# Attending in one accumulation bank, a longer rest in the gating, and key features made in blocks of 432 keys

## The chip, the core and the metric

The kernel runs on one core of a Trainium2 chip. The metric is the device time of one execution in microseconds (us). A core has five engines that run their own instruction streams: TensorE (PE, with its weight loads shown apart as PEld), VectorE (DVE), ScalarE (ACT), GpSimd (POOL) and SyncE (SP, which issues the transfers here). Matmuls write into PSUM, eight banks of 512 fp32 columns by 128 partitions; everything is fp32.

## What is computed

Eight images of 128 channels and 36 x 36 = 1296 positions go through two layers. The first is a convolutional attention with residual. The second is an additive attention over the 1296 tokens, followed by a layer of 64 experts which each take the 8 tokens they rate highest.

```python
def _L1_attn_ref(x, mask, Wq, bq, Wk, bk, w, bw):
    q = jnp.einsum('bld,ed->ble', x, Wq) + bq
    k = jnp.einsum('bld,ed->ble', x, Wk) + bk
    t = jnp.tanh(q[:, :, None, :] + k[:, None, :, :])
    scores = jnp.einsum('bijd,d->bij', t, w) + bw[0]
    attn = jax.nn.softmax(scores, axis=-1)
    return jnp.einsum('bij,bjd->bid', attn, x)
...
x = x + _L0_conv_ref(_gn(x), ...)
t = _to_tokens(x)
t = t + _L1_attn_ref(_ln_t(t), ...)
t = t + _L1_ffn_ref(_ln_t(t), ...)
```

The score of a query i and a key j is a sum over 128 channels of w times tanh(q + k). It isn't computed channel by channel. The kernel writes tanh through products of exponentials: over small groups of channels, a query and a key each get features exp(...), and the sum over a group is a quotient of two matrix products of these features.

## The kernel before

**The loop.** A *unit* is one key tile of 128 keys (11 tiles, the last of 16 keys) against one chunk of 432 queries (three chunks), for one image (called a batch here). A full unit has 12 *slots*, the unit of the 16-key tile has two; in all there are 2928 slots. A slot p does, in this order:

- `numerators(p)`: two products `n` into two banks of the PSUM pool `ps_n` (four banks);
- `denominators(p + 3)`: two products `d` into one of two pairs of banks of `ps_d`, then a Ln on ACT, and in every second slot an Exp over two slots' logarithms `lq` (the reciprocals);
- `terms(p)`: DVE multiplies `n` by `lq`. In slots 2, 5, 8 and 11 (`DVE_PAIRS`) DVE also adds the products up, in PSUM; in the other slots they go to SBUF as `rp`, and POOL adds them up.

Of three slots, two have products of 32 rows and the third (k = 2, 5, 8, 11) of 64 rows. The two halves of `n`, or of `d`, lie on different rows of the array.

**The work beside it.** Everything else is written as generators that stand in four lanes: `first_of_all` (features of queries, the scores of the 16-key tile), `urgent` (attending), `gates` (the expert gating of the batch before) and `background` (the next batch's first layer, its tokens and its key features). Each generator yields at the points where it may be interrupted: `matmuls(rest)` means that its next piece issues matmuls, and that it isn't taken up before `rest` slots have passed; `TAKE` means that its next piece takes a result out of PSUM, from the next slot on. `take_turns` runs pieces without matmuls at the start of a slot, except in `DVE_PAIRS` slots. `matmul_turn` runs at most one piece with matmuls at the end of a slot, and for the lanes other than `first_of_all` none in a slot just before a `DVE_PAIRS` slot, nor while the columns issued so far are ahead of 400 per slot (`PACE`). So the lanes get at most two turns in three slots. All of these take their PSUM banks from `ps_n` too, through `aux`. A bank is given out again in the program's order, and who gets it waits for its last reader. `exps` runs the `urgent` lane until it is empty when a chunk has its first exponentials and is about to get its second.

**Key features.** `keys` (L667) makes, for each key tile, eight matmuls of 128 columns (`NF` = 8), four to a bank, so two turns a tile; each bank gets one Exp of 512 columns on ACT (L687) into a tile `ks` (three buffers) and one write to the DRAM tensor `kd`, which holds a tile's features contiguously. For the 16-key tile POOL makes two masked copies (L692). `prefetch` (L932) loads a key tile's features as 4096 contiguous bytes per partition, two units ahead. In batch 0 the first tile is made before the loop straight into SBUF, two more tiles follow, and the others stand in the `urgent` lane.

**Attending.** When a chunk has all its exponentials `e`, `attend` forms the weighted sum over the 1296 keys for its four blocks of 108 queries: 11 matmuls a block. They are split into six and five. The first six go into a bank that DVE copies into SBUF (`sums`, L770), the other five into another bank, and DVE adds the two (L772). Then come a reciprocal, a scaling with addition (L775), and the statistics for the next normalization. For the very last chunk `attend_early` does nine of the eleven in the same way ahead of time.

**Gating.** `gate_logits` normalizes the tokens: DVE adds the epsilon (`ve`), two slots later POOL computes the inverse root `t_rs` (L265). Then come four transposes, a copy (L820), a rest of one slot, and two pairs of transposes back, which DVE scales with `t_rs` (L830).

Of the kernel before, what the change touches and what calls it, by code (L numbers as in the profile page):

```python
# [10 lines left out]
F32 = mybir.dt.float32  # L11
AF = mybir.ActivationFunctionType
ALU = mybir.AluOpType
# [3 lines left out]
N = H * W  # L17
# [53 lines left out]
def kernel(  # L71
# [41 lines left out]
        return t  # L113


    kd = [dram.tile([NKT, 128, NF * 128], F32, tag=f"kd{b % 2}", name=f"kd{b}") for b in range(NB)]
    tokd = [dram.tile([N, C], F32, tag=f"tokd{b % 2}", name=f"tokd{b}") for b in range(NB)]
    t2d = [dram.tile([C, N], F32, tag=f"t2d{b}", name=f"t2d{b}") for b in range(NB)]
    gd = [dram.tile([E, N], F32, tag=f"gd{b}", name=f"gd{b}") for b in range(NB)]
# [10 lines left out]
    with ExitStack() as loop, ExitStack() as score:  # L130
# [146 lines left out]
        def matmuls(rest=0):  # L277
            return (True, rest)
# [308 lines left out]
        prepared, made = {}, set()  # L587

        def tokens(b):

# [73 lines left out]
                nc.sync.dma_start(xr[32 * i : 32 * i + REM], xh[:REM, NKT - 1, :])  # L664
            prepared[b] = (xh, xT, xr)

        def keys(b, tiles):  # L667

            xT = prepared[b][1]
            yield matmuls(1)  # L670
            for t in tiles:
                o, n = KT[t]
                first = (b, t) == (0, order[0])
                if first:
                    kf_of[0] = kfp.tile([128, NF, 128], F32, tag="kf", name="kf")
                for q0 in (0, NF // 2):
                    some = slice(q0, q0 + NF // 2)
                    pk = aux("pk1").rearrange("p (q t) -> p q t", t=128)
                    for q in range(NF // 2):
                        bmm(pk[:, q, :n], a_k[:, (q0 + q) * 128 : (q0 + q + 1) * 128],  # L680
                           xT[:, o : o + n], start=True, stop=True)
                    yield TAKE
                    if first:
                        ks = kf_of[0][:, some, :]
                    else:
                        ks = kstp.tile([128, NF // 2, 128], F32, tag="ks", name="ks")
                    nc.scalar.activation(ks[:, :, :n], pk[:, :, :n], AF.Exp)  # L687
                    kd3 = kd[b][t].rearrange("p (q t) -> p q t", t=128)[:, some, :]
                    if n == REM:

                        for x in range(2):
                            nc.gpsimd.tensor_scalar(  # L692
                                ks[:, :, (x + 1) * n : (x + 2) * n], ks[:, :, :n],
                                pairs[:, min(q0, 1), x : x + 1], None, ALU.mult,
                            )
                        nc.sync.dma_start(kd3[:, :, : 2 * n], ks[:, :, n : 3 * n])
                    else:
                        nc.sync.dma_start(kd3, ks)
                    if q0 > 0:
                        made.add((b, t))  # L700
                    yield matmuls()

        def query_block(b, c, q, qf):

# [15 lines left out]
        def attend_early(b, c, es):  # L720

            xh, _, xr = prepared[b]
            held = [chunk_tile("sums") for _ in range(TPC // 2)]
            for i in range(TPC):
                at = (i % 2) * (C + 1)
                sums = early[i] = held[i // 2][:T, at : at + C + 1]
                for some in (order[:5], order[6 : NKT - 2] + order[5:6]):
                    pa = aux("pa1")[:T, : C + 1]
                    weigh(pa, i, some, es, xh, xr)
                    yield TAKE  # L730
                    if some[0] == order[0]:
                        nc.vector.tensor_copy(sums, pa)
                    else:
                        nc.vector.tensor_add(sums, pa, sums)
                    yield matmuls()

        def weigh(pa, i, some, es, xh, xr):

            for j in some:
                if j < NKT - 1:  # L740
                    e, v = es[j][:, i * T : (i + 1) * T], xh[:, j, :]
                else:
                    rows = slice(32 * i, 32 * i + REM)
                    e, v = es[j][rows, :T], xr[rows]
                bmm(pa, e, v, start=(j == some[0]), stop=(j == some[-1]))

        def attend(b, c, es):
# [11 lines left out]
            for i, at in enumerate(own):  # L759
                if i in early:  # L760
                    parts, sums = (order[NKT - 2 :],), early[i]
                else:
                    parts = (range(6), range(6, NKT))
                    sums = two.tile([T, C + 1], F32, tag="sums", name="sums")
                for some in parts:
                    pa = aux("pa1")[:T, : C + 1]
                    weigh(pa, i, some, es, xh, xr)
                    yield TAKE
                    if some[0] == 0:
                        nc.vector.tensor_copy(sums, pa)  # L770
                        yield matmuls()
                nc.vector.tensor_add(pa, pa, sums)  # L772
                inv = small.tile([T, 1], F32, tag="inv", name="inv")
                nc.vector.reciprocal(inv, pa[:, C : C + 1])
                nc.vector.scalar_tensor_tensor(  # L775
                    t2[:T, at, :], pa[:, :C], inv, t2[:T, at, :], ALU.mult, ALU.add
                )
                st = small.tile([T, 6], F32, tag="t2_st", name="t2_st")
                nc.vector.bn_stats(st, t2[:T, at, :])
                nc.vector.bn_aggr(mv[:, at, :], st)  # L780
                yield matmuls()
            if c == NCH - 1:
                prepared.pop(b)
            if b == NB - 1:
                yield from gate_logits(b, [c])
# [7 lines left out]
        def gate_logits(b, chunks):  # L793
# [23 lines left out]
            for c in chunks:  # L817
                tp, tt = turned(c, "t2T")
                yield TAKE
                nc.vector.tensor_copy(tt, tp[:, :CH])  # L820
                nc.sync.dma_start(t2d[b][:, c * CH : (c + 1) * CH], tt)
                yield matmuls(1)
                for j0 in range(0, TPC, 2):
                    tp = aux("tp3")
                    for j in (j0, j0 + 1):
                        turned_to(tp[:T, j * C : (j + 1) * C], tt[:, j * T : (j + 1) * T], ident)
                    yield TAKE
                    for j in (j0, j0 + 1):
                        t = c * TPC + j
                        nc.vector.tensor_scalar(  # L830
                            t2[:T, t, :], tp[:T, j * C : (j + 1) * C],
                            mv[:, t, 0:1], rs[:, t - tiles[0] : t - tiles[0] + 1],
                            ALU.subtract, ALU.mult,
                        )
                    yield matmuls()
# [90 lines left out]
        def prefetch(u):  # L926
            if u < len(units) and u not in kf_of:
                b, c, j = units[u]
                assert (b, j) in made
                n = 128 if j < NKT - 1 else 32  # L930
                kf = kfp.tile([128, NF, 128], F32, tag="kf", name="kf")
                nc.sync.dma_start(  # L932
                    kf[:, :, :n], kd[b][j].rearrange("p (q t) -> p q t", t=128)[:, :, :n]
                )
                kf_of[u] = kf

# [161 lines left out]
                next(aside, None)  # L1098
        drain(aside)
        a_q, a_k, cs_s, fb_s, eb_s = (feat[n] for n in ("a_q", "a_k", "cs_s", "fb_s", "eb_s"))  # L1100
        drain(tokens(0), keys(0, order[:1]))
        for i, q in enumerate(IN_TURN):
            if i < 3:
                drain(new_block(0, 0, q))
# [253 lines left out]
```

The softmax here doesn't subtract the row's maximum and nothing guards it: scores larger than these inputs give would overflow.

## Time and profile before

| | us |
|---|---|
| median of 3 runs (6137.38 to 6148.23) | 6137.45 |
| the profiled execution | 6140.74 |
| its span, first to last instruction | 6139.0 |
| POOL's additions `accp` of a slot (L1012), mean of one | 2.025 |
| DVE's products `rp` (L1003), mean of one | 0.600 |
| Exp of key features, 512 columns (L687), mean of one | 0.586 |
| Exp of key features, 64 columns (L687) | 0.205 |
| Exp of query features with bias, 432 columns (L710) | 0.608 |
| copy `sums` (L770), 92 of them | 0.289 |
| addition of `sums` (L772), 96 of them | 0.292 |

The loop's first slot starts about 162 us into the span and its last about 5985 us; the first layer of batch 0 lies ahead of it, and the experts' layer behind it. The mean granted clock of TensorE is 0.985 of full speed. The DMA engines are busy 13% of the time. A busy share is an average over the whole span; a line's last part names what ended the idle time ahead of its instructions.

### The profile page before, as it was taken

To read this page: it belongs to the slowest core of one execution; us is meant where nothing else is said; L and a number is where in the kernel's file an instruction comes from. 1 tells how busy PE (TensorE), PEld (TensorE's weight loads), DVE (VectorE), ACT (ScalarE), POOL (GpSimd) and SP (SyncE) were. 2 spreads that over 40 slices of the span, in tenths; PEclk is the share of its full clock that TensorE was granted. 3 is DMA by queue.
4 is the path that set the end of the run, shared out by engine and by line. 5 is a ranking of instruction groups with operands and counts; after the bars stand their busy time and mean duration, and the time that the engine had idled before them with its cause. 6 is when DMAs were issued, how large, how long until landed. Compare 5 with 4: busy or idle time off the path is not lost.

```text
span 6139.0 us, 93072 instructions
## 1 busy us (share of the span) xinstructions
PE 5957.9 (97%) x33480; PEld 2862.1 (47%) x33480; DVE 4796.4 (78%) x9521; ACT 5279.9 (86%) x5371; POOL 4597.7 (75%) x2819
## 2 busy tenths in 40 slices
PE   7999999999999999999999999999999999999996
PEld 5454444544544445444455444454444544544443
DVE  4787878877788787877888777887778877788882
ACT  1888898888988888889998889888898888999990
POOL 4777777777787777778778786877777777787870
PEclk9999999999999999999999999999999999999997
DMA  1210011100110002100111001110011100110008
GB/s 44 70 37 22 25 62 38 34 25 28 68 43 20 26 27 71 39 24 23 44 55 39 22 24 59 44 39 22 20 65 40 34 25 28 58 50 29 28 20 297
DMA packets 151519, 270.87 MB, mean 44 GB/s; under 512 B 45648, under 2 KB 76752, under 8 KB 151056
## 3 DMA queue, kind: packets, MB, share of 16 engines
q1 hardware_dynamic: 151056, 264.92, 13.0%
q8 instruction: 264, 4.33, 0.3%
q14 instruction: 199, 1.63, 0.1%
HBM read 200.41 MB, written 64.19 MB: 43 GB/s over the span
## 4 chain that ended last, share of the span: by engine, by line
PE 77%; ACT 7%; DVE 6%; issue 6%; POOL 2%; DMA 1%; SPq 0%; DVEq 0%; POOLq 0%; ACTq 0%
PE n L949 37%; PE d L949 12%; PE pa L284 7%; PE pc L284 5%; ACT lq L972 5%; PE s L284 3%; PE pk L284 3%; PE pq L284 3%; DVE rp L1003 2%; DVE n L997 1%; DVE accd L999 1%; PE d L954 1%; ACT lq L975 1%; DMA w<-in_weight_dram 1%; PE n L954 1%
## 5 line engine op out<-in xcount | busy, mean ns | idle before, releaser
L1012 POOL TENSOR_TENSOR accp<-accp,rp 128x864 f32<-128x864 f32 x1440 | 2915.8, 2025 | 1041.0 <-DVE rp L1003 948.8
L949 PE MATMUL n<-qf,kf 32*128 32x432 f32 (+1 forms) x11520 | 3325.3, 574 | 46.5 <-ACT e L1032 13.3
L949 PE MATMUL d<-qf,kf 32*128 32x432 f32 (+1 forms) x11520 | 2991.6, 561 | 38.7 <-ACT lq L972 38.2
L972 ACT ACTIVATE lq<-d 128x864 f32<-128x864 f32 x2928 | 2524.2, 878 | 542.6 <-PE d L949 512.1
L1003 DVE TENSOR_TENSOR rp<-n,lq 128x432 f32<-128x432 f32 x3912 | 2173.3, 600 | 743.5 <-PE d L949 542.8
L975 ACT ACTIVATE lq<-lq 128x1728 f32<-128x1728 f32 (+1 forms) x1464 | 2398.2, 1638 | 46.3
L949 PEld LDWEIGHTS n<-qf,kf 32*128 32x128 f32 (+1 forms) x11520 | 1206.4, 184 | 1600.3 <-DVE rp L1003 581.5
L949 PEld LDWEIGHTS d<-qf,kf 32*128 32x128 f32 (+1 forms) x11520 | 1090.0, 185 | 422.1 <-issue 224.7
L997 DVE TENSOR_TENSOR n<-n,lq 128x432 f32<-128x432 f32 x1440 | 814.9, 608 | 142.1 <-PE n L949 88.5
L999 DVE TENSOR_TENSOR accd<-n,accd 128x432 f32<-128x432 f32 x1440 | 866.3, 602 | 24.6
L1010 POOL TENSOR_TENSOR accp<-rp 128x864 f32<-128x864 f32 x240 | 485.2, 2022 | 197.7 <-DVE rp L1003 195.6
L711 POOL TENSOR_SCALAR qf<-qf,cs_s 128x432 f32<-128x432 f32 x192 | 260.9, 1365 | 45.0 <-ACT qf L710 44.4
L284 PEld LDWEIGHTS pa<-xh,e 128*108 128x108 f32 x1920 | 222.5, 174 | 131.1 <-DVE rp L1003 56.0
L1021 POOL TENSOR_TENSOR accd<-accp,accd 128x432 f32<-128x432 f32 x240 | 265.2, 1105 | 18.8
L1019 POOL TENSOR_TENSOR accp<-accp 128x432 f32<-128x432 f32 x240 | 264.4, 1102 | 16.7
L284 PE MATMUL pa<-xh,e 128*108 128x129 f32 x1920 | 262.9, 283 | 8.7 <-ACT e L1032 5.2
L284 PE MATMUL s<-q,k 128*116 128x432 f32 x480 | 230.3, 568 | 1.7 <-DVE q L316 1.4
L284 PEld LDWEIGHTS pk<-xT,a_k 128*128 128x128 f32 x1408 | 171.2, 192 | 107.0 <-DVE n L997 33.7
L462 POOL TENSOR_TENSOR tot<-tot,e 116x432 f32<-116x432 f32 x192 | 212.0, 1104 | 6.0 <-ACT e L471 4.6
L471 ACT ACTIVATE e<-s 116x432 f32<-116x432 f32 x240 | 124.9, 520 | 98.3 <-PE s L284 97.9
L284 PE MATMUL pa<-e,vw 116*128 116x432 f32 x480 | 204.6, 549 | 0.0
L284 PE MATMUL pk<-xT,a_k 128*128 128x128 f32 (+1 forms) x1408 | 202.5, 287 | 0.1
(213 smaller groups left out, 3788.4 us busy)
## 6 DMA issues: line engine op xcount, KB each, us to landing
kf<-kd SPq DMA_DIRECT2D x239, 512.0 KB
kd<-ks SPq DMA_DIRECT2D x158, 256.0 KB
w<-in_weight_dram SPq DMA_DIRECT2D x32, 1024.0 KB
wk_t<-wk_t_d SPq DMA_DIRECT2D x7, 768.0 KB
wv_t<-wv_t_d SPq DMA_DIRECT2D x7, 768.0 KB
wq_t<-wq_t_d SPq DMA_DIRECT2D x7, 768.0 KB
x<-in_x_dram SPq DMA_DIRECT2D x8, 648.0 KB
t<-tokd SPq DMA_DIRECT2D x96, 54.0 KB
```

What stands on the lines that cost most here:

```text
L284: mm(out, lhsT, rhs, **kw)
L711: nc.gpsimd.tensor_scalar(qf[:, 1, :], qf[:, 0, :], cs_s[:, q : q + 1], None, ALU.mult)
L949: mm(outs[h][:, :CH], kf[rows[h], q, :], qf_of[b, c, q][rows[h], part, :], start=True, stop=True)
L972: nc.scalar.activation(lq[:, o : o + n, :], d[:, :n, :CH], AF.Ln)
L975: nc.scalar.activation(some, some, AF.Exp, scale=-1.0)
L997: mult(ns[h], ns[h], lq[:, o + h, :])
L999: nc.vector.tensor_add(live["d"], ns[h], live["d"])
L1003: mult(rp[:, h, :], n, lq[:, o + h, :])
L1010: nc.gpsimd.tensor_add(live["p"], live["r"], rp)
L1012: nc.gpsimd.tensor_add(live["p"], live["p"], rp)
L1019: nc.gpsimd.tensor_add(s[:, 0, :], s[:, 0, :], s[:, 1, :])
L1021: nc.gpsimd.tensor_add(d, s[:, 0, :], d)
```

## The change

There are three edits.

1. Key features are made by `keys(b, lo, hi)` for a block of up to 432 keys: eight matmuls of the block's width, one to a bank, each a turn of its own with its own Exp and its own write. `kd` becomes `[128, NF, N]`, with the keys along the row, so that a tile's load has pieces of 512 bytes. The two masked copies of the last 16 keys are made per feature group into a tile `kr`, and go to a DRAM tensor of their own, `krd`. In batch 0 the blocks are 128, 384, 384, 16 and 384 keys.
2. Attending's 11 matmuls of a block accumulate in one bank, in turns of four, four and three; the bank is held from the first turn to the scaling. The copy and the addition of `sums` are gone (for the last chunk, early sums are copied once, and added once).
3. In the gating, the rest between the first chunk's copy and its transposes back is four slots instead of one (batch 7 excepted).

```diff
-    kd = [dram.tile([NKT, 128, NF * 128], F32, tag=f"kd{b % 2}", name=f"kd{b}") for b in range(NB)]
+    kd = [dram.tile([128, NF, N], F32, tag=f"kd{b % 2}", name=f"kd{b}") for b in range(NB)]
+    krd = [dram.tile([128, NF, 2 * REM], F32, tag=f"krd{b % 2}", name=f"krd{b}") for b in range(NB)]
...
-        def keys(b, tiles):
+        def keys(b, lo, hi):
...
+            n = hi - lo
+            first = b == 0 and lo == 0
...
+            for q in range(NF):
+                pk = aux("pk1")[:, :n]
+                bmm(pk, a_k[:, q * 128 : (q + 1) * 128], xT[:, lo:hi], start=True, stop=True)
+                yield TAKE
+                ks = kf_of[0][:, q, :] if first else kstp.tile(
+                    [128, CH], F32, tag="ks", name="ks")[:, :n]
+                nc.scalar.activation(ks, pk, AF.Exp)
+                nc.sync.dma_start(kd[b][:, q, lo:hi], ks)
+                if hi == N:
+
+                    for x in range(2):
+                        nc.gpsimd.tensor_scalar(
+                            kr[:, q, x, :], ks[:, n - REM :],
+                            pairs[:, q // (NF // 2), x : x + 1], None, ALU.mult,
+                        )
+                yield matmuls()
+            if hi == N:
+                nc.sync.dma_start(krd[b], kr.rearrange("p q x t -> p q (x t)"))
...
         def weigh(pa, i, some, es, xh, xr):
-            for j in some:
+            for x, j in enumerate(some):
...
-                bmm(pa, e, v, start=(j == some[0]), stop=(j == some[-1]))
+                last = x == len(some) - 1
+                bmm(pa, e, v, start=(x == 0), stop=last)
+                if last:
+                    yield TAKE
+                elif x % 4 == 3:
+                    yield matmuls()
...
             for i, at in enumerate(own):
+                pa = aux("pa1")[:T, : C + 1]
+                yield from weigh(pa, i, order[NKT - 2 :] if i in early else order, es, xh, xr)
                 if i in early:
-                    parts, sums = (order[NKT - 2 :],), early[i]
-                else:
-                    parts = (range(6), range(6, NKT))
-                    sums = two.tile([T, C + 1], F32, tag="sums", name="sums")
-                for some in parts:
-                    pa = aux("pa1")[:T, : C + 1]
-                    weigh(pa, i, some, es, xh, xr)
-                    yield TAKE
-                    if some[0] == 0:
-                        nc.vector.tensor_copy(sums, pa)
-                        yield matmuls()
-                nc.vector.tensor_add(pa, pa, sums)
+                    nc.vector.tensor_add(pa, pa, early[i])
...
-                yield matmuls(1)
+                yield matmuls(1 if c > chunks[0] or b == NB - 1 else 4)
...
-                    kf[:, :, :n], kd[b][j].rearrange("p (q t) -> p q t", t=128)[:, :, :n]
+                    kf[:, :, :n], kd[b][:, :, o : o + n] if j < NKT - 1 else krd[b]
...
-        drain(tokens(0), keys(0, order[:1]))
+        drain(tokens(0), keys(0, 0, 128))
...
-        drain(keys(0, order[1:3]))
+        drain(keys(0, 128, 512))
         prefetch(1)
-        urgent.append(keys(0, order[3:]))
+        for lo, hi in ((512, 896), (N - REM, N), (896, N - REM)):
+            urgent.append(keys(0, lo, hi))
...
-                            (normal(b + 1), conv_keys(b + 1), layer0(b + 1), tokens(b + 1),
-                             keys(b + 1, range(NKT)))
+                            (normal(b + 1), conv_keys(b + 1), layer0(b + 1), tokens(b + 1))
+                            + tuple(keys(b + 1, o, o + CH) for o in range(0, N, CH))
```

More of the change, by code (lines that the diff above doesn't have):

```diff
@@ L585, in features @@
             feat.update(cs_s=cs_s, fb_s=fb_s, eb_s=eb_s)
-        prepared, made = {}, set()
+        prepared, made, covered = {}, set(), {}
         def tokens(b):
@@ L665, in tokens @@
             prepared[b] = (xh, xT, xr)
-        def keys(b, tiles):
+        def keys(b, lo, hi):
             xT = prepared[b][1]
-            yield matmuls(1)
[L671 to L681, printed above, removed]
-                    yield TAKE
-                    if first:
-                        ks = kf_of[0][:, some, :]
-                    else:
[L686 to L700, printed above, removed]
-                    yield matmuls()
@@ new lines, in keys @@
+            n = hi - lo
+            first = b == 0 and lo == 0
+            if first:
+                kf_of[0] = kfp.tile([128, NF, 128], F32, tag="kf", name="kf")
+            if hi == N:
+                kr = one.tile([128, NF, 2, REM], F32, tag="kr", name="kr")
+            yield matmuls(1)
+            for q in range(NF):
[13 more added lines that the diff above has]
+                yield matmuls()
@@ L703, in query_block @@
+            if hi == N:
+                nc.sync.dma_start(krd[b], kr.rearrange("p q x t -> p q (x t)"))
+            done = covered.setdefault(b, set())
+            done.update(range(lo, hi))
+            made.update((b, t) for t, (o, m) in enumerate(KT) if done.issuperset(range(o, o + m)))
         def query_block(b, c, q, qf):
@@ L726, in attend_early @@
                 sums = early[i] = held[i // 2][:T, at : at + C + 1]
-                for some in (order[:5], order[6 : NKT - 2] + order[5:6]):
-                    pa = aux("pa1")[:T, : C + 1]
-                    weigh(pa, i, some, es, xh, xr)
-                    yield TAKE
-                    if some[0] == order[0]:
-                        nc.vector.tensor_copy(sums, pa)
-                    else:
-                        nc.vector.tensor_add(sums, pa, sums)
-                    yield matmuls()
+                pa = aux("pa1")[:T, : C + 1]
+                yield from weigh(pa, i, order[: NKT - 2], es, xh, xr)
+                nc.vector.tensor_copy(sums, pa)
+                yield matmuls()
         def weigh(pa, i, some, es, xh, xr):
-            for j in some:
+            for x, j in enumerate(some):
                 if j < NKT - 1:
@@ L744, in weigh @@
                     e, v = es[j][rows, :T], xr[rows]
-                bmm(pa, e, v, start=(j == some[0]), stop=(j == some[-1]))
+                last = x == len(some) - 1
[3 more added lines that the diff above has]
+                elif x % 4 == 3:
+                    yield matmuls()
         def attend(b, c, es):
@@ L759, in attend @@
             for i, at in enumerate(own):
+                pa = aux("pa1")[:T, : C + 1]
+                yield from weigh(pa, i, order[NKT - 2 :] if i in early else order, es, xh, xr)
                 if i in early:
-                    parts, sums = (order[NKT - 2 :],), early[i]
-                else:
-                    parts = (range(6), range(6, NKT))
-                    sums = two.tile([T, C + 1], F32, tag="sums", name="sums")
-                for some in parts:
-                    pa = aux("pa1")[:T, : C + 1]
-                    weigh(pa, i, some, es, xh, xr)
-                    yield TAKE
-                    if some[0] == 0:
-                        nc.vector.tensor_copy(sums, pa)
-                        yield matmuls()
-                nc.vector.tensor_add(pa, pa, sums)
+                    nc.vector.tensor_add(pa, pa, early[i])
                 inv = small.tile([T, 1], F32, tag="inv", name="inv")
@@ L931, in prefetch @@
                 kf = kfp.tile([128, NF, 128], F32, tag="kf", name="kf")
+                o = KT[j][0]
                 nc.sync.dma_start(
-                    kf[:, :, :n], kd[b][j].rearrange("p (q t) -> p q t", t=128)[:, :, :n]
+                    kf[:, :, :n], kd[b][:, :, o : o + n] if j < NKT - 1 else krd[b]
                 )
```

## The prediction

> **What bounds the kernel now.** I read the page's busy shares first, then the waits, then windows over single units of work, then the timeline. [...]
>
> ```profile
> PE 5957.9 (97%) x33480; PEld 2862.1 (47%) x33480; DVE 4796.4 (78%) x9521; ACT 5279.9 (86%) x5371; POOL 4597.7 (75%) x2819
> ACT lq L972 <- PE d L949: 512.1, 665, 3.3
> L972 ACT ACTIVATE lq<-d 128x864 f32<-128x864 f32 x2928 | 2524.2, 878 | 542.6 <-PE d L949 512.1 <-PE d L954 12.4 <-PE n L949 6.6
> L975 ACT ACTIVATE lq<-lq 128x1728 f32<-128x1728 f32 (+1 forms) x1464 | 2398.2, 1638 | 46.3
> ```
>
> PE's 97% counts pipelined ends and is no measure of PE at its peak. ACT has a Ln in each slot and an Exp in every second one, and nearly all of its idle time in the loop is one wait: Ln for the denominators `d`, 512 us. So ACT sets the pace, and each us in which PE brings `d` late is lost. Where that happens is seen in windows (us, busy time by engine PE, PEld, DVE, ACT, POOL, then clock and DMA):
>
> ```profile
> 5619.14:5639.08 19.94, 19.24 (x98) 7.67 (x96) 16.71 (x32) 19.75 (x20) 16.76 (x10) 1.00 0.05 9
> 1592.70:1617.81 25.11, 25.11 (x155) 13.73 (x154) 17.09 (x32) 23.93 (x28) 16.21 (x10) 1.00 0.29 103
> 5562.35:5593.89 31.54, 30.92 (x208) 18.43 (x208) 27.34 (x62) 26.08 (x26) 22.37 (x13) 1.00 0.06 18
> 952.64:979.70 27.06, 25.48 (x117) 10.93 (x117) 22.76 (x47) 21.18 (x21) 21.05 (x12) 0.81 0.10 37
> 1690.94:1714.69 23.75, 22.20 (x117) 10.82 (x116) 22.29 (x47) 20.51 (x20) 19.39 (x12) 1.00 0.12 42
> ```
>
> In order: a quiet unit (ACT full, 1.66 us a slot); a unit with keys' turns (ACT idle 1.2 us); the 15 slots of one attending (idle 5.5 us); the unit with the gating's root in batch 1 (idle 5.9 us, clock 0.81) and in batch 2 (idle 3.2 us). The root's stall, on the timeline (start, us, engine, line):
>
> ```profile
> 957.55 2.29 POOL L265 TENSOR_TENSOR t_rs<-ve,neg_half 108x12 f32<-108x12 f32 x1
> 959.88 0.73 DVE L830 TENSOR_SCALAR t<-tp,t_mv,t_rs 108x128 f32<-108x128 f32 x2 [0.89 <-POOL t_rs L265]
> 960.66 2.11 PE L949 MATMUL n<-qf,kf 32*128 32x432 f32 x3 [1.19 <-DVE t L830]
> 963.58 0.89 ACT L972 ACTIVATE lq<-d 128x864 f32<-128x864 f32 x1 [2.66 <-PE d L949]
> ```
>
> DVE waits 0.89 us for the root, PE 1.19 us for the banks behind DVE, ACT 2.66 us. And one kind of slot, where the second bank of `n` comes late, beside the same slot undisturbed:
>
> ```profile
> 5566.86 0.99 PE L949 MATMUL n<-qf,kf 64*128 64x432 f32 x4
> 5567.69 0.89 PE L949 MATMUL d<-qf,kf 64*128 64x432 f32 x4
> 5568.51 1.13 PE L284 MATMUL pa<-xh,e 128*108 128x129 f32 x8
> ...
> 5578.63 1.14 PE L949 MATMUL n<-qf,kf 64*128 64x432 f32 x3
> 5579.46 0.52 PE L949 MATMUL d<-qf,kf 64*128 64x432 f32 x1
> 5579.61 0.52 PE L949 MATMUL n<-qf,kf 64*128 64x432 f32 x1
> 5579.82 1.04 PE L949 MATMUL d<-qf,kf 64*128 64x432 f32 x3
> 5580.79 1.58 PE L284 MATMUL pa<-xh,e 128*108 128x129 f32 x12
> ```
>
> Undisturbed: 5566.86 to 5568.51, 1.65 us. With the late bank: 5578.63 to 5580.79, 2.16 us.
>
> [...] a late half of `n` loses its partner and holds `d` behind it, 0.51 us in the slots above. [...] 0.81 of the clock in that unit, the 432-column matmul 0.93 us instead of 0.53. [...] 8 matmul records of 111 ns, start to start, make 0.89 us, and such a turn took 1.07 us (5568.51 to 5569.58). [...] The trace has 27 ns for a 512-byte packet and 159 ns for 4096 bytes, 1.4 times as long per byte.
>
> **The change part by part.**
>
> Gating's root. Three slots more (5 to 6 us) between the copy of `t2T` and the transposes that need `t_rs`. In the new order POOL makes one 2.02 us addition and two small ones ahead of the root, so that is about 2.7 us later; it needs 0.89 us plus that. The wait goes, with some 2 us to spare. The units concerned took 27.1, 23.8, 27.3, 24.5, 25.4, 23.7 and 23.9 us in batches 1 to 7 (175.7 us). Without the stall and the half clock I take 22.8 us, as of the unit before each (23.0), since the turns moved out land in later units: 7 x 22.8 = 159.6. Gain 16 us; bounds 8 (only the half clock's part, what is over 23.75) and 24.
>
> Keys by blocks, batches 1 to 7. Removed per batch: 20 turns of 1.09 us on PE [...] and 2 of about 0.9: 23.6 us. Added: 24 turns of 2 x 0.362 us (the start-to-start time of pq's 432-column records) [...]: 19.7 us. ACT: 20 x 0.587 + 2 x 0.205 = 12.2 us becomes 24 x 0.525 = 12.6 us (Ln and Exp of 432 columns took 0.52). ACT is the bound there, so PE's 3.9 us buy only ACT's idle time: 1.2 us a unit in 2.75 units, 3.2 us, of which I take 2.7, less 0.4 of added Exp. Gain 2.3 a batch, 16 us in all. POOL's 16 multiplications of 16 columns (0.33 us each, an estimate from 446 ns for 64 columns and 1365 for 432) are 5.2 us where 1.8 were, beside POOL's 16.2 of 25.1 us: hidden. Loads of keys in 512-byte pieces take 1.7 us of the DMA engines' time instead of 1.3, and are issued over one unit ahead of use: hidden. SP gets two writes more a batch, at 0.32 us: hidden, and uncovered they would cost under 1 us a batch.
>
> Keys, batch 0. The head makes eight Exps of 384 columns through three buffers whose writes take 2.1 us to come back (the fourth Exp now waits 1.17 us for that): about 3 us more before the loop. Then the 24 single turns don't fit before the second `exps`, which drains the lane: in the new order ten of them stand in one slot. Ten at 0.85 us, with 4.7 us of it ACT's own Exps: about 4 to 5 us lost. Cost 8 us; bounds 3 and 14.
>
> Attending. Removed per token block: a copy (289 ns) and an addition (292 ns) on DVE[...]. Added: a third turn. A turn of four is 1.07 us, of three 0.85: 2.99 a block against 1.51 + 1.07 = 2.58; four blocks 12.0 against 10.3 us. With at most two turns in three slots, 12 turns take 18 slots where 8 took 15. Holding a bank leaves three for `n`, whose second bank then waits for the first product of the slot before. The order shows this wait all through. Behind a turn DVE has the time (0.94 + 1.07 us against 1.65); where a slot without a turn comes ahead of a 64-row slot, and the bank isn't just free, `n` is late: four times in 18 slots, 0.55 us each. So: 6 x (0.94 + 0.94 + 1.65) = 21.2, turns 12.0, the wait ahead of the first turn 1.1 as now, late banks 2.2: 36.5 us. Before: 31.5 and three quiet slots (3 x 1.66), 36.5 us. Net 0. Bounds for the 24 attendings: +36 if the three slots would have run at PE's own 1.18 us; -50 if no bank is late. What queues behind the waiting half of `n` is `d` of three slots on, and for that ACT.
>
> The tail has one more turn of one matmul: under 0.5 us.
>
> Sum against the profiled execution (6140.7 us around a span of 6139.0): -16 - 16 + 8 + 0 = -24, 6117. The median of the runs lies 3.3 us lower: 6113 us.
>
> **Rivals.**
> (a) Slower: the held bank. Place: `n`'s second bank in the 18 slots of each attending. Price 0.5 us per late half. It decides from two more late halves per attending on (24 x 1.0 = 24 us); if every slot after a turnless or an interrupted one is late, about five more, it gives +60, 6173 us. For it: n already waits 581 us in all for DVE's products. Against: in PE-bound stretches DVE is done early, and it loses 0.58 us per block.
> (b) Larger gain: turns of at most eight records no longer starve ACT, and half of the 5.5 us idle goes: -2 us x 24, 6065 us. For it: ACT's idle follows the 12-record turns (1.43 us after the one at 5570.76). Against: PE's work per attending grows.
> (c) Nothing to be measured: batch 0 costs 14 and keys gain nothing, since ACT is the bound: -16 + 14 = -2, 6136 us.
>
> **How the numbers follow.** Forecast 0.50 (most of its spread is below 6125), (a) 0.27, (b) 0.12, (c) 0.11. A change within 0.2% (12 us) can't be told from none. Faster: 0.44 + 0.12 = 0.56; within: 0.06 from the forecast, 0.02 from (a), 0.09 from (c), 0.17; slower: 0.25 + 0.02 = 0.27. The forecast's own range is 6090 to 6132; over all cases 6065 to 6175.
>
> **What would show it.** DVE's scaling of `t` waits no more for `t_rs`, and clocks near 0.81 vanish from those units: else the root's step is wrong. Keys' units near 24 us with ACT idle under 0.5 us; one stretch of 8 us in unit 2 of batch 0 with ten keys' turns. An attending's 18 slots near 36.5 us, with 2.16 us slots; 39 or more would be (a), 34 or less (b). The total is wrong if attending moves by over 1 us a time.

## The result and the profile after

The changed kernel takes 6209.85 us (median of 4 runs, 6207.53 to 6212.01) where the kernel before takes 6137.43. The ratio is 1.0113, 95% interval 1.0096 to 1.0131: about 72 us slower. The forecast was 6113.

The page of the changed kernel, the lines that answer to those of before (busy time by engine; then Ln and Exp with busy time, mean ns, idle time ahead and its releasers):

```profile
PE 6007.4 (97%) x32488; PEld 2759.1 (44%) x32488; DVE 4763.4 (77%) x9333; ACT 5281.3 (85%) x5403; POOL 4620.6 (74%) x2915
L963 ACT ACTIVATE lq<-d 128x864 f32<-128x864 f32 x2928 | 2521.4, 878 | 587.1 <-PE d L940 528.9
L966 ACT ACTIVATE lq<-lq 128x1728 f32<-128x1728 f32 (+1 forms) x1464 | 2398.2, 1638 | 46.3
```

ACT's work is the same to 2 us, and its idle time ahead of Ln grew from 542.6 to 587.1 us: the loop lost 49 us, nearly all of it as ACT waiting. The wait for `d` alone explains only 17 of these 45 us, so the page does not say where. The windows do (columns as in the prediction; quiet unit, keys unit, the 18 slots of the attending that took 15 before, the gating's unit 2 in batches 1 and 2):

```profile
5662.22:5682.06 19.84, 19.18 (x97) 7.68 (x96) 16.27 (x31) 19.65 (x20) 16.80 (x10) 1.00 0.05 8
1602.40:1626.74 24.34, 24.34 (x113) 9.92 (x113) 18.26 (x34) 24.07 (x28) 17.29 (x10) 1.00 0.26 86
5600.62:5640.45 39.83, 39.29 (x233) 21.05 (x233) 31.00 (x64) 32.34 (x31) 27.74 (x15) 1.00 0.05 15
964.70:985.34 20.64, 20.12 (x109) 9.46 (x108) 20.25 (x45) 19.06 (x19) 17.30 (x11) 1.00 0.30 106
1704.17:1725.92 21.75, 21.50 (x112) 9.02 (x111) 20.56 (x45) 19.60 (x20) 17.91 (x13) 1.00 0.35 118
```

The same 18 slots of the kernel before:

```profile
5562.35:5598.96 36.61, 35.94 (x232) 20.91 (x232) 32.24 (x75) 31.09 (x30) 25.42 (x14) 1.00 0.05 15
```

Keys and gating look as forecast: the keys unit takes 24.34 us with 0.3 us of idle ACT, unit 2 takes 20.6 and 21.75 us at a clock of 1.00. Attending takes 39.83 us instead of 36.61, above the 39 that the prediction gave as the mark of rival (a). Inside one attending of the changed kernel (timeline: start, us, engine, line, operation, count, idle time before):

```profile
5604.77 1.36 PE L940 MATMUL n<-qf,kf 64*128 64x432 f32 x3
5605.50 0.18 PEld L940 LDWEIGHTS n<-qf,kf 64*128 64x128 f32 x1 [0.44 <-DVE rp L994]
5605.60 0.54 PE L940 MATMUL d<-qf,kf 64*128 64x432 f32 x1
5605.97 0.52 PE L940 MATMUL n<-qf,kf 64*128 64x432 f32 x1
5605.97 1.24 PE L940 MATMUL d<-qf,kf 64*128 64x432 f32 x3
5607.15 0.47 PE L285 MATMUL pa<-xh,e 128*108 128x129 f32 x2
5607.25 0.89 ACT L963 ACTIVATE lq<-d 128x864 f32<-128x864 f32 x1 [1.00 <-PE d L940]
5607.55 0.47 PE L285 MATMUL pa<-xr,e 16*108 16x129 f32 x2
5607.94 0.69 PE L285 MATMUL pa<-xh,e 128*108 128x129 f32 x4
5608.56 0.63 PE L940 MATMUL n<-qf,kf 32*128 32x432 f32 x2
```

Two things stand here. The last half of `n` comes late, released by DVE's `rp`: the slot's own work takes 5604.77 to 5607.15, 2.38 us instead of 1.65, and ACT waits 1.00 us for `d`. And the second turn runs from 5607.15 to 5608.56, 1.41 us for eight records that were priced at 1.07: the 16-row tile `xr` stands in its middle. The two pairs of records ahead of a change of rows (128 to 16, and 16 to 128) take 0.40 and 0.39 us from start to start, where two records in a run take 0.22 (twice the 0.111 of the prediction): 0.35 us more.

A second loss is behind the loop. The tail (from the start of the loop's last slot to the end of the span) grew from 153.9 to 169.3 us:

```profile
6040.62 1.52 SPq L1170 DMA_DIRECT2D w<-in_weight_dram  x3
6044.82 0.17 DVE L764 RECIPROCAL inv<-pa 108x1 f32<-108x1 f32 x1
6060.15 5.57 SPq L757 DMA_DIRECT2D t<-tokd  x4
6070.50 0.35 DVE L765 SCALAR_TENSOR_TENSOR t<-pa,inv,t 108x128 f32<-108x128 f32 x1 [25.51 <-DMA t<-tokd]
```

DVE has everything for the last attending at 6044.99 but the tokens, and waits 25.51 us for them. Their four loads are issued behind nine loads of the experts' weights (only the first of those lines is shown). `urgent.run(len(slots))` takes up one piece of the urgent lane ahead of the weights; in the kernel before this piece is `attend`'s first, with the token loads in it (in its trace SP issues them from 5923.32 us on, 64 us ahead of the first weights). In the changed kernel `attend_early` has three turns where it had two, one of its pieces is still left, and that is what is taken up.

The span grew by 67.4 us. To see where, the starts of `n` were read from the trace for every slot. An attending's *window* is taken as 30 slots, from slot 6 of unit 0 to the end of unit 2, because what the 18 slots lose or gain is partly made good in unit 2 (23 attendings lie in the loop; their 18 slots took 36.5 us on average before and 39.2 after):

| us | head | 23 windows | rest of the loop | tail |
|---|---|---|---|---|
| before | 161.9 | 1394.0 | 4429.3 | 153.9 |
| after | 164.7 | 1419.8 | 4452.6 | 169.3 |
| difference | +2.9 | +25.8 | +23.3 | +15.4 |

The four differences make up the 67.4 us. The rest of the loop was to become shorter, and became longer, with no attending in it.

### The profile page after: what moved, and what is told of

Same layout as the page of the kernel before. It is cut to its first block, busy times and chain, and to the rows that moved or that the text cites. A ratio compares the mean times of both kernels' runs of the same rounds, so it can differ in the third digit from the quotient of the medians.

```text
span 6206.4 us, 91193 instructions
## 1 busy us (share of the span) xinstructions
PE 6007.4 (97%) x32488; PEld 2759.1 (44%) x32488; DVE 4763.4 (77%) x9333; ACT 5281.3 (85%) x5403; POOL 4620.6 (74%) x2915
## 4 chain that ended last, share of the span: by engine, by line
PE 80%; ACT 7%; issue 5%; DVE 4%; POOL 2%; DMA 1%; SPq 0%; DVEq 0%; POOLq 0%; ACTq 0%
PE n L940 41%; PE d L940 12%; PE pa L285 8%; PE pc L285 5%; ACT lq L963 5%; PE s L285 3%; PE pk L285 3%; PE pq L285 3%; DVE rp L994 1%; DVE n L988 1%; ACT lq L966 1%; PE d L945 1%; DMA w<-in_weight_dram 1%; PE n L945 1%; PE px L285 1%
## 5 line engine op out<-in xcount | busy, mean ns | idle before, releaser
L963 ACT ACTIVATE lq<-d 128x864 f32<-128x864 f32 x2928 | 2521.4, 878 | 587.1 <-PE d L940 528.9
L285 PE MATMUL pa<-xh,e 128*108 128x129 f32 x1920 | 310.3, 292 | 7.3 <-ACT e L1023 4.1
L285 PE MATMUL pk<-xT,a_k 128*128 128x432 f32 (+3 forms) x416 | 192.8, 554 | 2.4 <-ACT ks L685 2.4
L285 PE MATMUL pq<-xT,a_q 128*128 128x432 f32 x384 | 190.0, 577 | 0.4 <-DVE rp L994 0.4
```

Of the source, the lines that this page charges most:

```text
L285: mm(out, lhsT, rhs, **kw)
L963: nc.scalar.activation(lq[:, o : o + n, :], d[:, :n, :CH], AF.Ln)
```

## The experiments

Each is timed beside runs of the kernel before, whose medians lay at 6133 to 6139 us. "Window", "rest" and "tail" are the sums above, read from each kernel's own trace. A unit is written (batch, chunk, tile), a slot (batch, chunk, tile, slot).

| kernel | us | ratio, 95% interval | windows | rest | tail |
|---|---|---|---|---|---|
| e1_gating | 6187.8 | 1.0081 (1.0069 to 1.0094) | 1387.8 | 4482.9 | 154.5 |
| e2_keys | 6150.7 | 1.0019 (1.0012 to 1.0026) | 1403.7 | 4426.9 | 155.0 |
| e3_attend | 6253.8 | 1.0187 (1.0173 to 1.0201) | 1434.3 | 4488.2 | 163.0 |
| e4_tail | 6199.4 | 1.0100 (1.0084 to 1.0115) | 1419.7 | 4455.3 | 156.1 |
| e5_last | 6215.1 | 1.0124 (1.0109 to 1.0139) | 1397.9 | 4490.4 | 165.4 |
| e6_nohold | 6181.6 | 1.0070 (1.0055 to 1.0085) | 1369.2 | 4486.2 | 154.6 |
| e7_held65 | 6149.3 | 1.0021 (1.0012 to 1.0029) | 1406.6 | 4432.9 | 153.9 |
| e8_rest6 | 6135.6 | 0.9996 (0.9987 to 1.0005) | 1368.5 | 4448.6 | 156.3 |
| e9_ag | 6205.4 | 1.0110 (1.0095 to 1.0125) | 1427.8 | 4453.0 | 164.3 |
| e10_dev | 6179.1 | 1.0064 (1.0047 to 1.0082) | 1391.8 | 4455.5 | 154.0 |
| e11_rest2 | 6130.0 | 0.9988 (0.9981 to 0.9995) | 1382.4 | 4431.9 | 154.8 |
| e12_rest5 | 6192.2 | 1.0090 (1.0075 to 1.0105) | 1355.1 | 4518.7 | 154.8 |
| e13_best | 6138.6 | 1.0006 (0.9998 to 1.0014) | 1363.1 | 4456.8 | 157.2 |
| e14_all | 6129.9 | 0.9996 (0.9988 to 1.0004) | 1355.0 | 4453.4 | 155.5 |
| e15_mend | 6166.5 | 1.0055 (1.0039 to 1.0070) | 1396.4 | 4450.2 | 157.1 |
| e16_lane | 6123.7 | 0.9977 (0.9967 to 0.9987) | 1350.4 | 4447.6 | 157.2 |

### Each edit alone

The first theory: attending and the tail carry the loss, gating and keys gain as forecast. e1_gating is one line of the change:

```diff
-                yield matmuls(1)
+                yield matmuls(1 if c > chunks[0] or b == NB - 1 else 4)
```

> The kernel before with the rest of four slots in the gating alone. Theory A (the loss comes from attending and the tail, and the gating's step of the prediction is right): 16 us faster, about 6121 us, bounds 8 to 24; the units (b, 0, 2) near 22.8 us instead of 23.7 to 27.3. Theory B (the rest only moves the turns into later units, where they cost as much): within 4 us of before, with the units (b, 0, 3) to (b, 0, 6) longer by what unit 2 gained.

e2_keys is `keys`, `kd`, `krd` and the three places that call `keys`, with the loads from `kd` and `krd`, as in the change.

> The kernel before with keys by blocks alone (DRAM layout, loads and writes included). Theory A: -16 us in batches 1 to 7, +8 us in batch 0 and ahead of the loop, so about 6129 us, 6120 to 6140. Theory B (keys by blocks are the loss: batch 0, the writes' buffers, or the loads in 512-byte pieces): 6150 us or more, with ACT idle ahead of ks or PE waiting for kf.

e3_attend is `attend`, `attend_early` and `weigh` as in the change.

> The kernel before with attending in one held bank in turns of four alone. Theory A: 18 slots of an attending take 39.8 us instead of 36.6 (read from the changed kernel's trace), +3.2 x 24 = +77, and the tail +14 for the token loads that are issued behind the weights: about 6228 us, 6210 to 6240. Theory B (attending is neutral as predicted, and the loss is in keys or the gating): 6137 to 6155 us.

e4_tail is the changed kernel with

```diff
-        urgent.run(len(slots))
+        for _ in range(2):
+            urgent.run(len(slots))
```

> The changed kernel, with one more piece of the urgent lane taken up ahead of the experts' weights, so that the last chunk's four token loads (t<-tokd) are issued before the nine weight loads and not behind them. Theory A: DVE's wait of 25.5 us for t<-tokd goes, and the tail falls from 161.6 us to about 147.8 as before: 14 us faster than the changed kernel's 6209.9, about 6196 us. Theory B (the tail is set by the weights' arrival or by the half clock anyway): 6205 us or more.

The expectation counts the tail from a point 6.1 and 7.7 us behind the last slot's start, so its 147.8 and 161.6 us are 153.9 and 169.3 here. e4_tail came 10.5 us below the changed kernel, its tail at 156.1 us: the token loads are most of the tail's loss. e2_keys cost 12 us. Its time is at the edge of theory B, without that theory's signs: ACT was idle 5.0 us in all for the buffers of `ks`, and no wait of PE for `kf`'s loads shows. e3_attend is worse than expected, and e1_gating, forecast to gain 16 us, lost 49. The three edits alone sum to 49 + 12 + 115 = 176 us, the whole change costs 72. They do not add up, and the first theory fell for the gating.

### Inside attending

e5_last holds the bank, with the 16-key tile at the end of its block (in `attend_early` too):

```diff
-                yield from weigh(pa, i, order[NKT - 2 :] if i in early else order, es, xh, xr)
+                yield from weigh(pa, i, order[NKT - 2 :] if i in early else range(NKT), es, xh, xr)
```

> Attending alone as in e3_attend, held in one bank in turns of four, but with the 16-key tile last in its block instead of in the middle of the second turn. Theory A (the second turn takes 1.41 us instead of 1.07[...]): 96 x 0.35 = 34 us faster than e3_attend's 6253.8, about 6220 us. Theory B (only the held bank costs): 6248 us or more.

e6_nohold keeps before's banks and sums, with three parts:

```diff
-                    parts = (range(6), range(6, NKT))
+                    parts = (range(4), range(4, 8), range(8, NKT))
...
+                    elif some[-1] == 7:
+                        nc.vector.tensor_add(sums, pa, sums)
+                        yield matmuls()
```

> The kernel before with attending in turns of four, four and three, each in a bank of its own that DVE copies or adds into the sums as before: three turns a block, the 16-key tile last, and no bank held. It stands in the same slots as e3_attend. Theory A (half of attending's loss is the held bank, 24 x 1.8 = 43 us of late second halves of n): 43 us below e5_last, about 6177 us. Theory B (the third turn is the loss, the hold costs nothing): within 10 us of e5_last.

e7_held65 is e5_last with one interruption, behind the sixth matmul, instead of one behind every fourth.

> The kernel before with its turns of six and five, but both into one held bank, without the copy and the addition of sums. Every turn stands in the same slot as before. Theory A (the hold costs, because n has three banks left): 20 to 40 us slower than before, 6158 to 6178 us. Theory B (the hold costs nothing, the third turn does): 6125 to 6145 us.

Against 6220 and 6177 expected, e5_last and e6_nohold took 6215.1 and 6181.6 us. The 16-key tile in the middle costs 38.7 us, the hold 33.5, of which 10.8 are the tail by the traces (without a hold `attend_early` is as before, and so is the order of the loads). All three stand in the same slots, and the rest of the loop is 4486 to 4490 us in each. The hold is seen in the same slot of e5_last

```profile
5618.25 1.36 PE L940 MATMUL n<-qf,kf 64*128 64x432 f32 x3
5619.45 0.52 PE L940 MATMUL n<-qf,kf 64*128 64x432 f32 x1
5619.46 1.24 PE L940 MATMUL d<-qf,kf 64*128 64x432 f32 x3
5620.63 1.14 PE L284 MATMUL pa<-xh,e 128*108 128x129 f32 x8
```

and of e6_nohold:

```profile
5591.44 1.00 PE L952 MATMUL n<-qf,kf 64*128 64x432 f32 x4
5592.27 0.89 PE L952 MATMUL d<-qf,kf 64*128 64x432 f32 x4
5593.09 1.14 PE L284 MATMUL pa<-xh,e 128*108 128x129 f32 x8
```

With the bank held 2.38 us pass before the turn, without it 1.65. In this attending four 64-row slots are late so, by 0.73 to 0.84 us. With two turns a block (e7_held65) the hold cost 11 us, net of the copy and the addition that it saves, less than the 20 to 40 expected; a block's two turns lie nearer together, but that this is the reason was not tried.

Without hold and with the tile last, three short turns are no loss at all: the windows of e6_nohold are 24.8 us shorter than before's. Yet it lost 43 us (33 in the profiled execution, the fastest of its four), because the rest of the loop is 57 us longer. What an edit moves had become the larger question.

### Where later turns fall

e8_rest6, e11_rest2 and e12_rest5 are e1_gating with a 6, a 2 and a 5 for the 4. e9_ag is e3_attend with the rest of four.

> The kernel before with a rest of six slots in the gating instead of one; with it the turns come one permitted slot later than with four. Theory A (a longer rest in itself costs what e1_gating showed): 6185 us or more. Theory B (e1_gating's loss of 48 us is the place on which the later turns fall, of the 12 slots of a unit, and not the rest; the root's stall is gone in both): anything clearly different from e1_gating's 6187.8, by 20 us or more; between 6110 and 6165 us.

> The kernel before with a rest of two slots in the gating (the transposes back begin in slot 3 of unit 2 instead of slot 2). Theory A (time follows from the rest's length, as it hides the root): between before and e8_rest6's 6135.6, within 5 us of 6137. Theory B (the place of the later turns decides): any time from 6115 to 6190; the units of chunks 1 and 2 tell, which should be those of before, since in e8_rest6 too the later turns came back to their old places.

> The kernel before with a rest of five slots (the transposes back begin in slot 6 of unit 2). Theory A (length of the rest): between e1_gating's 6187.8 (four) and e8_rest6's 6135.6 (six), so near 6162 us. Theory B (places): the units of chunks 1 and 2 either keep before's times to 0.1 us, and then the total is 6125 to 6145 us, or are all shifted, and then it is off by tens of us.

> Attending in one held bank together with the rest of four slots, keys as before. Additive effects (e1_gating's +49 on e3_attend's 6253.8): about 6303 us. The prediction's view of the rest (-16 whatever stands around it): about 6238 us. Theory of places (the rest's worth depends on which slots the later turns fall on, and three more slots of attending shift them again): close to the changed kernel less keys' 12 us, about 6198 us, 6185 to 6215.

A rest of 1, 2, 4, 5 and 6 slots gives 6137, 6130, 6188, 6192 and 6136 us. No theory of the length of the rest gives this, and none of these edits adds an instruction. The units of chunk 2 in batch 5 (us, in the order in which the tiles run, and the chunk's sum), from the starts of the slots:

```
rest 1  25.7 23.7 24.8 26.2 21.9 4.3 23.2 20.7 25.3 25.1 26.8  247.9
rest 2  25.7 23.6 24.8 26.1 21.9 4.3 23.2 20.7 25.3 25.1 26.8  247.7
rest 6  25.7 23.6 24.8 25.7 21.9 4.3 23.2 20.7 25.3 25.1 26.8  247.3
rest 4  24.4 24.6 23.4 26.6 25.4 4.3 22.6 22.9 25.3 25.1 26.7  251.2
rest 5  23.9 23.6 23.7 30.5 21.7 4.3 24.6 21.1 25.3 25.1 26.8  250.8
```

With 2 and 6 the later turns come back to the places that they had, and every unit does too. With 4 and 5 they stand in other slots, up to the unit of tile 6 in chunk 2, with other times, although nothing is done there that wasn't done before.

The granted clock has a part in this. In the traces TensorE ran at half clock (granted clock 0.50) in the loop for 89, 72 and 58 us with rests of one, two and six slots, and for 133 and 154 us with four and five. Over all runs the mean clock is 0.985 to 0.989 with the first three and 0.979 to 0.983 with the other two. What such a stretch costs shows in e12_rest5, in the units (1, 1, 5), (2, 1, 5) and (3, 1, 5), which do the same work (columns as in the prediction):

```profile
1274.20:1300.56 26.36, 24.69 (x154) 11.81 (x152) 19.03 (x37) 21.44 (x23) 12.32 (x7) 1.00 0.06 21
2016.46:2045.88 29.42, 27.75 (x155) 12.73 (x153) 19.04 (x37) 21.44 (x23) 12.33 (x7) 0.88 0.06 19
2760.91:2787.27 26.36, 24.69 (x155) 11.81 (x153) 19.03 (x37) 21.44 (x23) 12.33 (x7) 1.00 0.07 21
```

The unit (1, 1, 5) of the kernel before:

```profile
1272.86:1297.40 24.54, 24.54 (x150) 12.49 (x148) 19.08 (x37) 21.12 (x22) 13.61 (x7) 1.00 0.08 26
```

The other places alone cost 1.8 us in this unit, and 6.8 us at half clock add 3.1. At that price (an estimate from these lines) the 44 and 65 us that e1_gating and e12_rest5 spend more at half clock than the kernel before make some 20 and 30 us of their 49 and 55 us. What starts such a stretch was not tried. The changed kernel's own loss is not the clock: in its loop PE spent 44 us at half clock, where it spent 89 before.

Beside the held attending the same rest of four gains 48 us (e9_ag): attending's three more slots had moved the turns, and the rest moves them again, to better places. Little of that is unit 2 itself: in batches 1 to 6 these units take 129.9 us in e3_attend and 123.8 in e9_ag (129.4 in the changed kernel).

One bad place was followed to its cause. e1_gating, in batch 5, where a pair of transposes stands in slots 11 and 0:

```profile
3948.57 2.01 POOL L1012 TENSOR_TENSOR accp<-accp,rp 128x864 f32<-128x864 f32 x1 [1.70 <-DVE gm L359]
3948.72 1.88 DVE L362 SCALAR_TENSOR_TENSOR dev<-dev,gn_mv 128x1 f32<-128x1 f32 x1
3952.59 1.24 DVE L999 TENSOR_TENSOR accd<-n,accd 128x432 f32<-128x432 f32 x2
3953.24 0.75 PE L949 MATMUL n<-qf,kf 32*128 32x432 f32 x1 [0.56 <-DVE accd L999]
3954.80 0.89 ACT L972 ACTIVATE lq<-d 128x864 f32<-128x864 f32 x1 [2.40 <-PE d L949]
```

A DVE instruction on 128 single elements (`dev`, of the next batch's normalization) takes 1.88 us: it ends at 3950.60, when POOL's addition ends (3950.58). That puts DVE's four instructions on `n` late; with one bank taken by the transposes, the next `n` waits for the last of them, `d` comes behind it, and ACT waits 2.40 us. e10_dev takes `dev` from PSUM:

```diff
-            nc.vector.tensor_sub(dev, mv[:, 0:1], gm)
-            nc.vector.scalar_tensor_tensor(dev, dev, dev, mv[:, 1:2], ALU.mult, ALU.add)
+            nc.vector.tensor_sub(pm[:, 1:2], mv[:, 0:1], pm[:, :1])
+            nc.vector.tensor_copy(dev, pm[:, 1:2])
+            nc.vector.scalar_tensor_tensor(dev, pm[:, 1:2], dev, mv[:, 1:2], ALU.mult, ALU.add)
```

> e1_gating with the next batch's variance of the group means (dev, L361 and L362) taken from PSUM, so that no DVE instruction there has two inputs in SBUF; everything else in the same order. Theory A (DVE's dev of 128x1 waits for POOL's addition of 2.0 us, which makes the pair of transposes behind it late): dev takes under 0.3 us instead of 1.88, the slot (b, 0, 3, 0) falls from 3.57 us to about 2.1 with 2.4 us of ACT's idle time, 7 times: about 15 us faster than e1_gating's 6187.8, 6173 us. Theory B (the pair stands in a bad slot whatever is ahead of it on DVE): 6183 us or more.

The same place in e10_dev:

```profile
3934.30 4.13 POOL L1013 TENSOR_TENSOR accp<-accp,rp 128x864 f32<-128x864 f32 x2 [3.02 <-DVE pm L361]
3934.52 0.22 DVE L363 SCALAR_TENSOR_TENSOR dev<-pm,dev,gn_mv 128x1 f32<-128x1 f32 x1
3938.45 0.89 ACT L973 ACTIVATE lq<-d 128x864 f32<-128x864 f32 x1 [0.32 <-PE d L950]
```

`dev` takes 0.22 us beside POOL, and ACT's wait is 0.32 us; the slot fell from 3.57 to 1.85 us. The place is explained. The median fell by 8.8 us where 15 were expected: in e1_gating the slot is not equally long in all seven batches (1.91 to 3.79 us), and over them e10_dev saves 7.6 us in it. The whole is less clear, for the intervals of the two kernels overlap: e10_dev's four runs lie between 6162 us at a mean clock of 0.986 and 6188 at 0.981. Its trace is that of the fastest, so its row in the table doesn't answer to its median.

### Prices and places together

With e13_best the sum was put to the test, and e14_all and e15_mend mend the change itself. e13_best is e6_nohold with the rest of four, e14_all adds keys by blocks, e15_mend is the changed kernel with e4_tail's and e5_last's edits.

> Attending in turns of four, four and three with a bank of its own for each turn (as e6_nohold), together with the rest of four slots; keys as before. Its turns stand in the slots of e9_ag. Theory of prices and places: the attendings' own slots as in e6_nohold (-24 us against before), the rest of the loop as in e9_ag (-6 us): about 6107 us, 6095 to 6120, faster than both kernels. Edits added up singly (e6_nohold +43, e1_gating +49): about 6231 us.

> As e13_best, with keys by blocks too: the changed kernel, but with separate banks for the three turns and the sums, the 16-key tile last, and the early sums as before. Theory of prices and places: attendings -24 us, the rest of the loop and the head as in the changed kernel (-12 and +3 us), tail as before: about 6104 us. If keys by blocks cost what e2_keys and the step from e9_ag to the changed kernel show (+4 to +12 us): 6111 to 6119 us.

> The changed kernel, still in one held bank, with the 16-key tile last in its block and the token loads ahead of the weights. If the two prices are independent of all else: 6209.9 - 38 - 10 = 6161 us, 6153 to 6170. If one of them only stood in for something else: 6180 us or more.

e15_mend took 6166.5 us (6161 expected): the two prices hold beside the other edits too. e13_best took 6138.6: far from the 6231 of single effects added, but 31 above the 6107 of prices and places. That sum had used windows of 18 slots. In these e9_ag loses 64 us against before, 30 of which it makes good by the end of unit 2, and the sum took these 30 for a gain of the rest of the loop; e6_nohold, with nothing to make good, has the same -25 us in either window. With windows of 30 slots, chosen after this result, it comes out: e6_nohold's windows (-24.8 against before) and e9_ag's rest (+23.7) make -1 us, and the medians differ by +5.5. e14_all lies 8.7 us below e13_best, above its figures for the same reason; keys by blocks cost nothing there. Five kernels with turns in these places (e9_ag, e13_best, e14_all, e15_mend, the changed kernel) have a rest of 4450 to 4457 us.

e14_all's batch 7 was still 13 us longer than before's. There the chunk's gate logits follow attending in the urgent lane, and with attending ending three slots later `exps` drains them in one slot. In the changed kernel, slot (7, 1, 2, 6), 5.54 us long:

```profile
5651.54 0.40 PE L289 MATMUL tp<-ident,t 108*128 108x108 f32 x2
5652.89 0.63 PE L289 MATMUL tp<-ident,t 108*128 108x108 f32 x2 [0.94 <-DVE t L820]
5654.22 0.94 PE L285 MATMUL pg<-xc,gate_w 128*64 128x432 f32 x2 [0.70 <-DVE xc L829]
```

e16_lane puts them into the lane of the gating:

```diff
-            if b == NB - 1:
+            if b == NB - 1 and c < NCH - 1:
+                gates.append(gate_logits(b, [c]))
+            elif b == NB - 1:
                 yield from gate_logits(b, [c])
```

> As e14_all, with the last batch's gate logits of chunks 0 and 1 in the gates lane instead of behind attending in the urgent lane, so that exps doesn't drain three of their turns in one slot (5.5 us in slot (7, 1, 2, 6) of the changed kernel). If that pile is what makes batch 7 of e14_all 13 us longer than before's: units (7, 1, 2) and (7, 2, 2) fall from 25.4 and 24.3 us to about 21, 8 us in all, about 6122 us against e14_all's 6129.9. If it isn't: 6127 us or more.

Units (7, 1, 2) and (7, 2, 2) fell to 21.0 us each, and the kernel to 6123.7 us, ratio 0.9977 (0.9967 to 0.9987): faster than both kernels.

## Why the prediction was wrong

- **Attending, "36.5 us before and after".** The failed step. Two terms of the sum were mis-sized. "A turn of four is 1.07" priced the number of records and not what is in them: the second turn of `order` has the 16-row tile in its middle and takes 1.41 us, 1.4 us an attending. "Late banks 2.2", four times 0.55, became 4.0 us in the attending shown, against the same slots undisturbed: four 64-row slots at 0.73 to 0.84 and two 32-row slots at about 0.4. The order had shown the wait; its price came from a slot of before that was late by 0.51 us. Rival (a) named the mechanism and its place, at 6173 us; it was set back because "in PE-bound stretches DVE is done early", and in the slots shown DVE wasn't.
- **Gating's root.** The stall went as forecast: no wait for `t_rs`, the clock at 1.00, unit 2 at 20.6 to 21.8 us (22.8 forecast). The step that failed is what it was said to be worth: "the turns moved out land in later units" at no cost. Alone they land where the kernel loses 49 us, though unit 2 itself gains 10 in the seven batches (e1_gating), and some 20 of the 49 are the clock's by the estimate above; with attending held, unit 2 had lost its stall already.
- **Keys, batches 1 to 7.** In place the gain was as forecast: the units 7 to 9 of chunk 2 are 17.4 us shorter in e2_keys in batches 1 to 6, 2.9 a batch (2.3 forecast). The forecast's 19.7 us a batch for PE's 24 turns held an estimate: such a turn took 0.92 us in the changed kernel (1603.34 to 1604.26), 22.1 us for 24. The gain is given back: 24 turns instead of 22 end later, and more of them run into the next batch (five instead of two). In batches 2 to 7 units 0 and 1 of chunk 0 are 11.8 us longer together and unit 2, with the root's stall, 8.1. The spill was not in the sum. Batch 0 and the head: 8 us forecast, 2.2 + 4.5 measured in e2_keys, with ten keys' turns in one slot as forecast (10.49 us in the changed kernel).
- **Tail, "under 0.5 us".** The second failed step: 15.4 us in the profile, of which e4_tail's profile takes back 13.2 and its median 10.5. PE's turns were counted, and the one piece that `urgent.run` takes up was not followed to the loads that it issues on SP's queue.
- **The form of the sum.** Four terms were added as if each stood alone. The runs show an interaction as large as the effects: the rest of four is +49 us in one kernel and -48 in another.

Open: for the places as a whole, only the slots of the later turns were varied, and one slot (e10_dev) and one pile of turns (e16_lane) were followed to a cause. The clock's part is an estimate. Which coincidences make up the other tens of us, and which of them bring a half clock with them, was not tried.

## What to carry to other kernels

In a loop whose side work is dealt out slot by slot, an edit has two prices: that of its own slots, and that of moving all later pieces; measure the second with an edit that only shifts them, read the granted clock beside it, and repeat a gain next to other edits before it is believed. Price a turn by what stands in it and not by its number of matmuls alone (eight records with the 16-row tile in their middle took 1.41 us here, eight of 128 rows 1.07), and an accumulation bank held over several turns by the producers that then wait for one bank less (33.5 us here with three turns a block, 11 with two, net of the copy and the addition saved). Where a piece of work is taken up once before a block of large loads, look at which piece it will be, and at what it issues.

## What the hardware showed unexpectedly

A DVE instruction on 128x1 elements with its inputs in SBUF (`dev`, L362) took 0.22 us where no instruction of POOL was under way (from 248.44, 982.67 and 2457.09 us on in the kernel before), and 0.96 to 1.15 us in its four other places in the loop there, each time ending 0.01 to 0.02 us behind an addition of POOL (L1021). In e1_gating it took 1.88 us and ended 0.02 us behind POOL's 2.01 us. With one of the inputs in PSUM it took 0.22 us beside POOL's addition (e10_dev). That is one instruction in three kernels; other operations and other places of the inputs were not tried.
